# A selective scan laid out with four states of 32 channels on the partitions instead of two states of 64

## The chip, the cores and the metric

The kernel runs on one core of a Trainium2 chip. The metric is the device time of one execution in microseconds (us), as the median of several runs; the core has five engines that matter here: TensorE (PE), VectorE (DVE), ScalarE (ACT), GpSimd (POOL) and the DMA engines, whose transfers SyncE (SP) issues. Tiles on the chip lie in SBUF or PSUM; in both kernels those that TensorE's matmuls write are the ones in PSUM.

## The reference, cut to what matters

A network of four layers on four images of 56 x 56 x 96. Nearly all of the time goes to the selective scan of layers 0 and 1: per image four directions over L = 3136 positions, for 192 channels and 16 states.

```python
def selective_ssm(dtw, dtb, xw, A_log, D, seq):
    xz = jnp.einsum('bld,kd->blk', seq, xw)
    dt_raw, b_ssm, c_ssm = ...                       # 12 (layer 1: 6), 16 and 16 columns of xz   [cut]
    dt = jax.nn.softplus(jnp.einsum('blr,dr->bld', dt_raw, dtw) + dtb)
    a = -jnp.exp(A_log)
    d_a = jnp.exp(dt[..., None] * a)
    d_b = dt[..., None] * b_ssm[:, :, None, :]
    def step(h, inp):
        da_t, db_t, x_t, c_t = inp
        h = da_t * h + db_t * x_t[..., None]
        y_t = jnp.einsum('bds,bs->bd', h, c_t)
        return (h, y_t)
    ...
    return jnp.swapaxes(ys, 0, 1) + seq * D
```

Per state and channel the work is an exp (`da`), a product (`dt*u` with B), a scan over positions (h), a product with C and a sum over the 16 states. Layer norms, convolutions, linear attention and an fp8 feed-forward surround it; the kernel runs them beside the scans of another image ("the other work" below).

## The kernel before

A sequence is cut into chunks of CS = 784 positions. A **unit** is one tile of 128 partitions: 64 channels (one of NG = 3 groups) by 2 states, for one chunk; 16 states make NQ = 8 units per group, 3072 units in all.

```python
    def spread_b(self, ch, q):                       # B of two states onto 128 partitions
        ps = self.psum.tile([128, 1024], F32, tag="b", name="b", bufs=2)
        w = self.sel[:, q].rearrange("p s d -> p (s d)")
        for s in (slice(0, 512), slice(512, CS)):
            self.nc.tensor.matmul(ps[:, s], w, ch.bc[:, s], start=True, stop=True)   # bf16, three terms
        return ps[:, :CS]
    ...
        for n, (ch, g, q) in enumerate(units):       # in scans()                           [cut]
            da = sp.tile([128, CS], F32, name="da", bufs=3)
            nc.scalar.activation(da, ch.dt[g], AF.Exp, scale=ch.na[:, g, q : q + 1])
            db = b
            nc.vector.tensor_tensor(db, ch.du[g], db, ALU.mult)          # in place in PSUM
            if n + 1 < len(units):
                b = self.spread_b(units[n + 1][0], units[n + 1][2])
            if late is not None:
                self.add_up(*late)
            hs = sp.tile([128, CS], F32, name="hs", bufs=2)
            at = ch.carry[:, g, q : q + 1]
            nc.vector.tensor_tensor_scan(
                hs[:, way], da[:, way], db[:, way], at if ch.step else 0.0, ALU.mult, ALU.add
            )
            if ch.step < NCS - 1:
                nc.scalar.copy(at, hs[:, end : end + 1])
            hc = sp.tile([128, CS], F32, name="hc", bufs=2)
            nc.gpsimd.tensor_tensor(hc, hs, ch.cc[q // 2][:, q % 2], ALU.mult)
            late = (ch, g, q, hc)
            yield ch                                 # the caller now emits a share of the other work
    ...
    def add_up(self, ch, g, q, hc):                  # sum over the states, in PSUM         [cut]
        for h in range(2):
            nc.tensor.matmul(
                self.y[64 * h : 64 * h + 64, :HC], self.two, hc[:, h * HC : (h + 1) * HC],
                start=q == 0, stop=False,
            )
```

The scan reads `da` from SBUF and `db` from PSUM.

## Time and profile before

| | before |
|---|---|
| time | 12854.27 us, median of 3 runs (12810.35 to 12864.53); 12832.31 with the run taken beside the change |
| head, loop of scans, tail | 147, 12127, 594 us |
| loop per three units ("a round" below) | 11.84 us |
| TensorE, VectorE, GpSimd, ScalarE busy | 83%, 70%, 54%, 51% |
| scan | 3072, mean 1.82 us |

Read it from the top down: the busy shares say that no engine is full; the groups say which instructions fill each engine and what their engine waited for; dividing the loop by 1024 gives the number that everything below is compared with. The lines themselves stand in the prediction.

### The profile page before, as it was taken

Reading aid. Unit: us, or ns where it says so; the run is one execution under the profiler, and the core shown is the slowest. Engines: PE = TensorE matmul, PEld = TensorE weight load, DVE = VectorE, ACT = ScalarE, POOL = GpSimd, SP = SyncE. Lnnn points to the kernel's source line nnn. Section 1 sums busy time; section 2 is a strip of 40 time slices with the busy share of each in tenths; the row PEclk is TensorE's granted clock in tenths of the full one; section 3 lists DMA queues with packets and bytes.
Section 4 is the critical chain, followed back from the end, with each engine's and each line's share of the span. In section 5 each row is a group of like instructions: output and inputs, shape, how many; then the busy total and the mean of one; then the engine's idle time right before and its main releaser. Section 6 shows DMA issues by size and latency. Waiting matters only on the chain. (4 is left out here: it accounts for less than half of the span.)

```text
span 12868.3 us, 101763 instructions
## 1 busy us (share of the span) xinstructions
PE 10724.2 (83%) x32510; PEld 3416.3 (27%) x32510; DVE 9010.8 (70%) x7546; ACT 6582.8 (51%) x10422; POOL 6985.7 (54%) x3964
## 2 busy tenths in 40 slices
PE   7888888987789878897889888888888888888786
PEld 3222122222223122231223223321233213332143
DVE  4776777667776777767776666877668776777722
ACT  4655555555555555555555544445444454445511
POOL 4555656556554665546555555556555565555510
PEclk6766667766667667776767677766777667776665
DMA  3221212112211221212222121211212122211110
GB/s 84 61 59 46 69 45 54 49 41 68 57 48 50 57 67 42 57 44 65 50 54 53 37 68 49 52 45 41 62 49 52 41 50 61 51 43 40 41 33 28
DMA packets 233374, 662.64 MB, mean 51 GB/s; under 512 B 60866, under 2 KB 141252, under 8 KB 231204
## 3 DMA queue, kind: packets, MB, share of 16 engines
q1 hardware_dynamic: 232064, 654.32, 20.6%
q8 instruction: 257, 4.21, 0.1%
q14 instruction: 281, 2.30, 0.1%
q10 hardware_dynamic: 772, 1.80, 0.1%
HBM read 548.41 MB, written 107.58 MB: 51 GB/s over the span
## 5 line engine op out<-in xcount | busy, mean ns | idle before, releaser
L537 POOL TENSOR_TENSOR hc<-hs,cc 128x784 f32<-128x784 f32 x3072 | 5704.9, 1870 | 4545.8 <-DVE hs L531 3550.0
L551 PE MATMUL y<-hc,two 128*64 128x392 f32 x12288 | 4120.3, 740 | 1294.4 <-POOL hc L537 1219.0
L524 DVE TENSOR_TENSOR b<-du,b 128x784 f32<-128x784 f32 x3072 | 2963.4, 970 | 2481.5 <-PE b L483 2468.6
L531 DVE TENSOR_TENSOR_SCAN hs<-da,carry,b 128x784 f32<-128x784 f32 x2304 | 4166.1, 1834 | 149.4 <-ACT da L522 91.7
L522 ACT ACTIVATE da<-dt,na 128x784 f32<-128x784 f32 x3072 | 2862.0, 945 | 728.9 <-DVE hs L531 714.1
L483 PE MATMUL b<-bc,sel 96*128 96x512 bf16 (+1 forms) x6144 | 2110.7, 436 | 489.9 <-DVE hs L531 486.3
L551 PEld LDWEIGHTS y<-hc,two 128*64 128x64 f32 x12288 | 839.8, 178 | 3117.3 <-POOL hc L537 2320.1
L535 ACT COPY carry<-hs 128x1 f32<-128x1 f32 x2304 | 431.8, 189 | 2140.9 <-DVE hs L531 2134.1
L531 DVE TENSOR_TENSOR_SCAN hs<-da,b 128x784 f32<-128x784 f32 x768 | 1346.3, 1774 | 54.4 <-ACT da L522 21.5
L483 PEld LDWEIGHTS <-sel 96*128 96x128 bf16 x6144 | 457.7, 108 | 3176.4 <-DVE hs L531 1322.1
L431 PE MATMUL ps<-U,wd 64*108 64x392 f32 (+1 forms) x1536 | 864.0, 774 | 0.0
L461 POOL TENSOR_TENSOR du<-dt,U 128x784 f32<-128x784 f32 x384 | 783.0, 2047 | 147.0 <-ACT dt L456 138.9
L593 POOL TENSOR_TENSOR rs<-rs,power 112x4 f32<-112x4 f32 x252 | 257.4, 1021 | 964.6 <-ACT rs L592 784.8
L455 PE MATMUL ps<-dtr,wd 12*128 12x392 f32 (+1 forms) x1536 | 752.5, 736 | 9.4 <-ACT dt L456 3.6
L652 PE MATMUL ps<-win,dg 64*64 64x220 f32 (+9 forms) x2016 | 689.5, 496 | 0.0
L522 ACT ACT_TABLE_LOAD x511 | 655.6, 1283 | 8.3
L568 ACT COPY Ya<-y 64x392 f32<-64x392 f32 x512 | 348.3, 680 | 550.8 <-PE y L565 476.6
L596 PE MATMUL ps<-ident,rs 112*96 112x112 f32 x2016 | 423.6, 376 | 202.8 <-POOL rs L593 202.0
L456 ACT ACTIVATE dt<-ps,wd 128x392 f32<-128x392 f32 x768 | 426.8, 585 | 288.8 <-PE ps L455 279.7
L456 ACT ACT_TABLE_LOAD x339 | 434.9, 1283 | 78.9 <-PE ps L455 73.7
L596 PEld LDWEIGHTS ps<-ident,rs 112*96 112x96 f32 x2016 | 349.2, 250 | 395.4 <-POOL rs L593 308.0
L652 PEld LDWEIGHTS ps<-win,dg 64*64 64x64 f32 (+2 forms) x2016 | 337.1, 175 | 353.9 <-issue 258.7
(215 smaller groups left out, 6739.9 us busy)
## 6 DMA issues: line engine op xcount, KB each, us to landing
cc<-cd SPq DMA_DIRECT2D x1024, 392.0 KB, 5.2
U<-u SPq DMA_DIRECT2D x64, 588.0 KB, 7.9
u<-w SPq DMA_DIRECT2D x56, 224.0 KB, 2.8
z<-w SPq DMA_DIRECT2D x56, 224.0 KB, 2.7
y<-Ya SPq DMA_DIRECT2D x8, 1568.0 KB, 7.0
w<-y SPq DMA_DIRECT2D x56, 224.0 KB, 3.9
w<-z SPq DMA_DIRECT2D x56, 224.0 KB, 4.0
wd<-in_wd_dram SPq DMA_DIRECT2D x32, 367.5 KB, 3.5
```

The source lines that it names most:

```text
L431: nc.tensor.matmul(ps[:m, :HC].rearrange("p (a b) -> p a b", b=HS), self.wx[rows, g, :m], self.in_order(self.U[rows, g], orient, c * CS + ...
L455: nc.tensor.matmul(ps[:, :HC], wt[rows, g], dtr[rows], start=True, stop=True)
L456: nc.scalar.activation(dt[:, h * HC : (h + 1) * HC], ps[:, :HC], AF.Softplus, bias=dtb[:, g : g + 1])
L461: nc.gpsimd.tensor_tensor(du.rearrange("p (a b) -> p a b", b=HS), ch.dt[g].rearrange("p (a b) -> p a b", b=HS), self.in_order(self.U[:, g] ...
L483: self.nc.tensor.matmul(ps[:, s], w, ch.bc[:, s], start=True, stop=True)
L522: nc.scalar.activation(da, ch.dt[g], AF.Exp, scale=ch.na[:, g, q : q + 1])
L524: nc.vector.tensor_tensor(db, ch.du[g], db, ALU.mult)
L531: nc.vector.tensor_tensor_scan(hs[:, way], da[:, way], db[:, way], at if ch.step else 0.0, ALU.mult, ALU.add)
L537: nc.gpsimd.tensor_tensor(hc, hs, ch.cc[q // 2][:, q % 2], ALU.mult)
L551: nc.tensor.matmul(self.y[64 * h : 64 * h + 64, :HC], self.two, hc[:, h * HC : (h + 1) * HC], start=q == 0, stop=False,)
L596: nc.tensor.matmul(ps[:, b], rs[:, q : q + 1].to_broadcast([NT, C]), self.ident[:NT, :NT], start=True, stop=True)
L652: self.nc.tensor.matmul(o[:, a - r0 : e - r0, x0:x1], diag[:, tap], win[:, a + dy - lo : e + dy - lo, x0 + dx : x1 + dx], start=n == 0, st ...
```

## The change

The intent is to relieve TensorE and to save instructions. A **round** now holds three tiles with 4 states of 32 channels each, which share one B and one C. So B is spread once for three tiles, C is multiplied in one instruction over all three, and the sums of the three tiles use three column blocks of 32 of the TensorE array; a fourth block is fed so that all four are in use, and its result is not read. `dt` and `du` are computed once per channel and copied onto the four state blocks by way of DRAM. One of the three products with B moves to GpSimd. Products, scans and product with C are all done in place in one SBUF tile `v`. There are 1024 rounds.

```diff
+    def spread(self, ch, e):
+        for n, l in ((0, ch.dt), (1, ch.du)):
+            t = self.sp.tile([128, NG, CS], F32, name="dt" if n == 0 else "du")
+            for s in range(4):
+                self.nc.sync.dma_start(
+                    t[32 * s : 32 * s + 32], ch.dd[e][n].rearrange("(g d) t -> d g t", d=32)
+                )
+            l.append(t)
     def spread_b(self, ch, q):
-        ps = self.psum.tile([128, 1024], F32, tag="b", name="b", bufs=2)
+        ps = self.psum.tile([128, 2, 512], F32, tag="b", name="b", bufs=1)
+        for h in range(2):
+            nc.tensor.matmul(ps[:, h, :HC], self.sel[:, h, q], ch.cf, start=True, stop=True)   # now fp32
+        b = self.sp.tile([128, CS], F32, name="bs", bufs=1)
+        nc.scalar.copy(b.rearrange("p (h t) -> p h t", h=2), ps[:, :, :HC])
+        return ps[:, :, :HC], b
... in scans():
+        def begin(n):
+            ch, e, q = rounds[n]
+            b, bs = self.spread_b(ch, q)
+            v = sp.tile([128, NG, CS], F32, name="v", bufs=3)
+            nc.gpsimd.tensor_tensor(v[:, 2], ch.du[e][:, 2], bs, ALU.mult)
+            return b, v
-            db = b
-            nc.vector.tensor_tensor(db, ch.du[g], db, ALU.mult)
+            for g in range(NG):
+                ...                                   # exp into das[g]
+                if g < 2:
+                    nc.vector.tensor_tensor(          # v[:, g] = du[:, g] * b
+                        v[:, g].rearrange("p (h t) -> p h t", h=2),
+                        ch.du[e][:, g].rearrange("p (h t) -> p h t", h=2), b, ALU.mult,
+                    )
+            if n + 1 < len(rounds):
+                nxt = begin(n + 1)
-            nc.vector.tensor_tensor_scan(
-                hs[:, way], da[:, way], db[:, way], at if ch.step else 0.0, ALU.mult, ALU.add
-            )
+            for g in range(NG):
+                nc.vector.tensor_tensor_scan(
+                    v[:, g, way], das[g][:, way], v[:, g, way], at[:, g : g + 1] if ch.step else 0.0, ALU.mult, ALU.add
+                )
-            nc.gpsimd.tensor_tensor(hc, hs, ch.cc[q // 2][:, q % 2], ALU.mult)
+            nc.gpsimd.tensor_tensor(v, v, cc.unsqueeze(1).to_broadcast([128, NG, CS]), ALU.mult)
... in add_up():
-            nc.tensor.matmul(
-                self.y[64 * h : 64 * h + 64, :HC], self.two, hc[:, h * HC : (h + 1) * HC],
-                start=q == 0, stop=False,
-            )
+            for n, g in enumerate((0, 1, 2, 2)):
+                nc.tensor.matmul(
+                    self.y[32 * n : 32 * n + 32, h, :HC], self.four, v[:, g, h * HC : (h + 1) * HC],
+                    start=q == 0 or n == 3, stop=n == 3,
+                )
... and: general PSUM tiles 3 -> 4; convolutions give way after every third tap; lengths 100, 260 -> 125, 275
```

## The prediction

> **What bounds the kernel now.** I read the page first: the busy shares, then the costliest groups.
>
> ```profile
> PE 10724.2 (83%) x32510; PEld 3416.3 (27%) x32510; DVE 9010.8 (70%) x7546; ACT 6582.8 (51%) x10422; POOL 6985.7 (54%) x3964
> ...
> L537 POOL TENSOR_TENSOR hc<-hs,cc 128x784 f32<-128x784 f32 x3072 | 5704.9, 1870 | 4545.8 <-DVE hs L531 3550.0
> L551 PE MATMUL y<-hc,two 128*64 128x392 f32 x12288 | 4120.3, 740 | 1294.4 <-POOL hc L537 1219.0
> L524 DVE TENSOR_TENSOR b<-du,b 128x784 f32<-128x784 f32 x3072 | 2963.4, 970 | 2481.5 <-PE b L483 2468.6
> L531 DVE TENSOR_TENSOR_SCAN hs<-da,carry,b 128x784 f32<-128x784 f32 x2304 | 4166.1, 1834 | 149.4 <-ACT da L522 91.7
> L522 ACT ACTIVATE da<-dt,na 128x784 f32<-128x784 f32 x3072 | 2862.0, 945 | 728.9 <-DVE hs L531 714.1
> ```
>
> The reader is to see a loop of 3072 units (exp, product with B, scan, product with C, sum) in which no engine is full. TensorE is nearest, at 83%; VectorE's long idle time ends on TensorE (its product waits 2468.6 us for the B broadcast), GpSimd's on the scan. So the bound is the in-order round trip PE, DVE, POOL, PE with TensorE as its fullest member. In the view of the scan's line the first scan starts at 147.1 us and the last at 12272.6: head 147 us, loop 12127 us, tail after the last scan 594 us. I count in rounds of three units, since the changed kernel works in them: 12127/1024 = 11.84 us per round. The chain of waits at its end spreads over many lines of 1% and names no single culprit.
>
> Then I asked the views of single lines what an instruction of VectorE costs beside GpSimd, because the change moves operands from PSUM to SBUF.
>
> ```profile
> L531 DVE TENSOR_TENSOR_SCAN hs<-da,carry,b x2304: 1811/1839/1850, 235.2 to 12272.6; 128x784 f32<-128x784 f32 x192
> ```
> ```profile
> L788 DVE TENSOR_TENSOR w<-w,ps x28: 602/605/614, 7545.9 to 12538.3; 64x448 f32<-64x448 f32 x28
> ```
> ```profile
> L704 DVE TENSOR_TENSOR w<-w x28: 588/608/2260, 1628.1 to 6782.2; 64x448 f32<-64x448 f32 x28
> ```
> ```profile
> L818 DVE SCALAR_TENSOR_TENSOR w<-w,c,win x28: 654/656/4555, 7596.3 to 12565.5; 96x448 f32<-96x448 f32 x28
> ```
>
> The numbers after the count are shortest, median and longest ns. The scan (da in SBUF, b in PSUM) and L788 (w in SBUF, ps in PSUM) never vary, though GpSimd is busy 54% of the time. L704 and L818, with both inputs in SBUF, take up to 2260 and 4555 ns. The timeline says where the 4555 comes from, VectorE first, then GpSimd in the same stretch:
>
> ```profile
> 7870.43 4.55 DVE L818 SCALAR_TENSOR_TENSOR w<-w,c,win 96x448 f32<-96x448 f32 x1
> ```
> ```profile
> 7869.85 1.01 POOL L593 TENSOR_TENSOR rs<-rs,power 112x4 f32<-112x4 f32 x1 [5.12 <-ACT rs L592]
> 7870.82 3.68 POOL L537 TENSOR_TENSOR hc<-hs,cc 128x784 f32<-128x784 f32 x2
> ```
>
> L818 starts while GpSimd works, stands through a power and two whole products until GpSimd ends at 7874.50, and ends 0.48 us after it: its own work alone. It is a lock, not a sharing of rate, and GpSimd keeps it from one instruction to the next if its queue is full.
>
> [...] This trace agrees for tensor_tensor and scalar_tensor_tensor (608 to 2260, 656 to 4555 ns); a scan with two SBUF inputs is not in it. [...] The trace has 1862 ns (median) for 784 elements[...]. [...] matmuls in different column groups run together. The trace agrees for two groups: 12288 L551 records of 740 ns would be 9.1 ms one after another and cover 4120.3 us.
>
> **The change part by part,** per round (three groups, one state quarter; 1024 rounds).
>
> TensorE. Sums: now four L551 records per unit cover 4120.3/3072 = 1.34 us, 4.02 per round. Then 16 records in fours; if four run together as two do now, 4 x 0.67 = 2.7 us. B: now 2110.7/1024 = 2.06 us per round in bf16; then two fp32 matmuls of 392 columns on the full array, 4 records of about 0.51 us (L609's 195.8 us over 336 records of 448 columns, scaled), 2.0 us: no gain. The projection goes from 12 to 8 records per chunk (864 to about 400 us in all), the step sizes from 6 matmuls to 4 (752 to 500 us). Sum: 10.7 - 1.35 - 0.1 - 0.45 - 0.25 = about 8.6 ms.
>
> ScalarE. Gone are the casts of B, cf and dtr copies (about 0.6 ms) and two thirds of the carries (432 to about 150 us); new are 1024 PSUM copies of 784 columns, about 0.8 us each (448 columns take 0.52[...]), 0.85 ms. About level at 6.5 ms.
>
> DMA. dt and du go to DRAM and back, four ways: 128 x 16 loads of 301 KB = 616 MB and 154 MB of stores onto 662 MB. The queue's share of 20.6% roughly doubles, issued a round or more ahead of use: hidden.
>
> VectorE, own work: 2 of 3 products stay, 2963 to 1976 us, the `rest` subtraction (140) goes: 9010 to about 7.9 ms.
>
> GpSimd, own work: the product with C as one of 2352 elements[...] instead of 3 x 1.86; plus one product with B, 1.86; plus two `du` products per chunk instead of three (256 x 2.04 = 0.52 ms), minus the bf16 correction (213 us). 7.12 us a round, about 8.1 ms in all.
>
> By these sums the fullest engine falls from 10.7 to 8.6 ms. But the scan now reads da and v, **both in SBUF**. If the lock holds for it, scans and GpSimd's instructions exclude each other and their times add:
> - three scans, started 1.74 us apart as in back-to-back pairs now (3.58 us for two, 1.84 for one): 5.2 us
> - product with C 5.26, product with B 1.86: 7.1 us
> - du: 0.52 ms/1024 = 0.51 us
> - the powers (257.4 us): 0.25 us
> - VectorE's other users[...] (L703, L704, L818, L862 and the fp16 steps at L853, L854, L861, unblocked about 226 us): 0.22 us
>
> Sum 13.3 us a round against 11.84 now. The two products from PSUM on VectorE (1.94 us) [...] hide under the C product; exps (2.8 us) and the B copy hide there too. I add 0.15 us for the handoff from scan to GpSimd, which waits for the last scan: 13.45 x 1024 = 13.77 ms, plus head and tail 0.74: **14.5 ms**, 13% slower.
>
> **Rivals.**
> A. The scan does not take the lock. At 1.84 us for 784 elements it runs at about half the rate of the product (0.97)[...] and no scan of this kind is in the trace. Then engines overlap, the fullest has 8.6 ms, and at today's 83% the time is 8.6/0.83 = 10.4 ms. For it speaks only that gap; against it, that two different opcodes with two SBUF inputs block for whole instructions.
> B. Lock plus stalls. B's PSUM tile has one buffer, so B for the next round starts after this round's products, then needs TensorE (2 us), the ScalarE copy (0.85) and the GpSimd product, behind convolutions and table loads (1283 ns each[...]). Where this arrives later than the scans end, nobody holds the lock. At 1 us a round: 15.6 ms.
> C. The lock, but cheaper: in blocked handoffs the fixed part is hidden (L818 needs 0.48 us after GpSimd instead of 0.66). With element time alone, scans 3 x 1.63 (an estimate: 1.84 less some 0.2 fixed)[...], rest 0.4: 12.5 us a round, 12.8 + 0.74 = 13.5 ms. Still slower.
> D. DMA or the one issuing queue holds it up: the spreads wait for stores that wait for GpSimd. They have a round of some 13 us for transfers that land in 5.2 us (392 KB) now; I give it little.
>
> **Range and chances.** B to C span 13.5 to 15.6 ms, and A is a separate heap at 10 to 11 ms to which I give 13%. I take 13.3 to 15.6 ms. Faster 0.14 (A), same 0.06 (all of C's savings and some of the scans slipping in unblocked), slower 0.80.
>
> **What would show it.** In the changed kernel the scan's mean rises far above 1.84 us, shortest near 1.75 and longest several us; GpSimd's product of 784 elements varies too. GpSimd's unblocked time plus unblocked scan time fills some 90% of the loop. TensorE's busy time falls to about 8.6 ms and yet nothing is gained. If the scan's shortest and longest are again within 0.1 us, the lock step is wrong and the time is A's. If scan and GpSimd times fit but the sum leaves over 1 us a round, it is B. If the sums at L551's successor cover clearly more than 2.7 us a round, four column groups do not run together.

## The result

| | before | changed |
|---|---|---|
| median | 12832.31 us (4 runs, 12782.0 to 12864.53) | 16234.17 us (4 runs, 16228.19 to 16246.59) |
| ratio | | 1.2657 (95%: 1.261 to 1.2704) |
| granted TensorE clock, profiled run | 0.689 | 0.666 |
| head and tail, loop | 741, 12127 us | 751, 15481 us |
| loop per round | 11.84 us | 15.12 us |
| mean scan | 1.82 us | 3.32 us |

The four runs of the kernel before lie within 0.7% of one another. A ratio here is worked out from the runs and not from the quoted medians, so it isn't quite their ratio.

The page of the changed kernel, first its busy shares, then the groups that answer to those of before (busy us, mean ns, then the idle time of the engine just before them and what ended most of it):

```profile
PE 9275.2 (57%) x33022; PEld 3530.1 (22%) x33022; DVE 12479.8 (77%) x6273; ACT 5525.5 (34%) x7879; POOL 9306.5 (57%) x2680
...
L560 DVE TENSOR_TENSOR_SCAN v<-da,carry,v 128x784 f32<-128x784 f32 x2304 | 7528.1, 3317 | 165.6 <-ACT da L548 139.3
L568 POOL TENSOR_TENSOR v<-v,cc 128x2352 f32<-128x2352 f32 x1024 | 5917.5, 5780 | 355.6 <-ACT carry L566 219.7
L521 POOL TENSOR_TENSOR v<-du,bs 128x784 f32<-128x784 f32 x1024 | 2367.9, 2312 | 4045.7 <-ACT bs L485 2842.3
...
L584 PE MATMUL y<-v,four 128*32 128x392 f32 x16384 | 2719.9, 745 | 2916.4 <-POOL v L568 2301.8
L483 PE MATMUL b<-cf,sel 128*128 128x392 f32 x4096 | 2571.4, 770 | 2499.7 <-DVE v L551 2499.6
L551 DVE TENSOR_TENSOR v<-du,b 128x784 f32<-128x784 f32 x2048 | 1885.0, 959 | 1605.9 <-ACT bs L485 761.0
```

Here the reader sees TensorE fall from 10724 to 9275 us of work, as intended, and VectorE rise to 12480 us although it has fewer instructions. The rise sits in one place: 2304 scans with carry that took 4166 us now take 7528. TensorE's new waits end on GpSimd's product (L568) and on VectorE's (L551); it isn't the bound any more.

The views of the scan's and the C product's line give the shortest, median and longest duration of one instruction, in ns:

```profile
L560 DVE TENSOR_TENSOR_SCAN v<-da,carry,v x2304: 1812/1840/12768, 261.2 to 15629.7; 128x784 f32<-128x784 f32 x192
...
L560 DVE TENSOR_TENSOR_SCAN v<-da,v x768: 1756/1783/8884, 150.3 to 15311.1; 128x784 f32<-128x784 f32 x192
```
```profile
L568 POOL TENSOR_TENSOR v<-v,cc x1024: 5122/5161/11168, 155.7 to 15631.6; 128x2352 f32<-128x2352 f32 x171
```

The median scan is as it was (1840 ns against 1839), and the longest is seven times as long. So the scan isn't slower; some scans stand. The timeline shows where, in an ordinary stretch (start us, duration us, engine, instruction):

```profile
5012.84 11.73 DVE L560 TENSOR_TENSOR_SCAN v<-da,carry,v 128x784 f32<-128x784 f32 x3
5012.94 6.69 POOL L568 TENSOR_TENSOR v<-v,cc 128x2352 f32<-128x2352 f32 x1
...
5019.60 3.33 POOL L521 TENSOR_TENSOR v<-du,bs 128x784 f32<-128x784 f32 x1
...
5026.24 5.32 DVE L560 TENSOR_TENSOR_SCAN v<-da,carry,v 128x784 f32<-128x784 f32 x3
```

In the second round three scans run with GpSimd idle and take 5.32 us. In the first they take 11.73 us, 6.41 more, because GpSimd's two products, 5.16 + 1.88 us of own work by their medians, take their turns between them (7.04 us, less some overlap at the handoffs). GpSimd's 6.69 and 3.33 us in turn are longer than its own work since it stands behind a scan. What one engine does here, the other waits for.

To account for a round I laid the instructions of the trace over one another. "Held" is the time in which a scan, another of the VectorE instructions that the last term of the prediction's sum counts, or a GpSimd instruction is running or standing; "idle" is the rest; and "alone" (from the experiments 11 to 14) is the middle of a pass from which the other work has been moved away.

| per round, us | held | idle | sum |
|---|---|---|---|
| predicted | 13.3 | 0.15 | 13.45 |
| changed kernel | 12.73 | 2.39 | 15.12 |
| changed kernel, rounds alone | 12.34 | 1.13 | 13.48 |

The waits of the changed kernel (us in total, times, longest) name first what lets the lock lie idle most: the copy of B into SBUF.

```profile
ACT da L548 <- DVE v L560: 5082.3, 1433, 12.2
...
POOL v L521 <- ACT bs L485: 2842.3, 478, 12.4
...
DVE v L551 <- ACT bs L485: 761.0, 290, 15.2
```

ScalarE waits 5082 us for scans to free the `da` tiles, which costs little: the scans in turn wait for `da` only 215.5 us (139.3 and 76.2). GpSimd's 2842 us lie mostly beside scans; only 684 us of them lie where the lock is idle. The next largest part of the idle lock, 508 us, ends on ScalarE's bias instruction before GpSimd's power (run 7).

### The profile page after: what moved, and what is told of

It reads as the page before. It is cut to its first block, busy times and chain, and to the rows that moved or that the text cites. A ratio compares the mean times of both kernels' runs of the same rounds, so it can differ in the third digit from the quotient of the medians.

```text
span 16232.6 us, 103602 instructions
## 1 busy us (share of the span) xinstructions
PE 9275.2 (57%) x33022; PEld 3530.1 (22%) x33022; DVE 12479.8 (77%) x6273; ACT 5525.5 (34%) x7879; POOL 9306.5 (57%) x2680
## 3 DMA queue, kind: packets, MB, share of 16 engines
q1 hardware_dynamic: 631424, 1399.75, 34.4%
## 5 line engine op out<-in xcount | busy, mean ns | idle before, releaser
L560 DVE TENSOR_TENSOR_SCAN v<-da,carry,v 128x784 f32<-128x784 f32 x2304 | 7528.1, 3317 | 165.6 <-ACT da L548 139.3
L568 POOL TENSOR_TENSOR v<-v,cc 128x2352 f32<-128x2352 f32 x1024 | 5917.5, 5780 | 355.6 <-ACT carry L566 219.7
L521 POOL TENSOR_TENSOR v<-du,bs 128x784 f32<-128x784 f32 x1024 | 2367.9, 2312 | 4045.7 <-ACT bs L485 2842.3
L584 PE MATMUL y<-v,four 128*32 128x392 f32 x16384 | 2719.9, 745 | 2916.4 <-POOL v L568 2301.8
L483 PE MATMUL b<-cf,sel 128*128 128x392 f32 x4096 | 2571.4, 770 | 2499.7 <-DVE v L551 2499.6
L551 DVE TENSOR_TENSOR v<-du,b 128x784 f32<-128x784 f32 x2048 | 1885.0, 959 | 1605.9 <-ACT bs L485 761.0
L560 DVE TENSOR_TENSOR_SCAN v<-da,v 128x784 f32<-128x784 f32 x768 | 2519.6, 3329 | 76.2 <-ACT da L548 76.2
L483 PEld LDWEIGHTS b<-cf,sel 128*128 128x128 f32 x4096 | 1052.0, 282 | 4041.2 <-issue 3818.1
L485 ACT COPY bs<-b 128x784 f32<-128x784 f32 x1024 | 821.3, 802 | 1077.2 <-PE b L483 1047.9
L453 POOL TENSOR_TENSOR duc<-dtc,U 96x784 f32<-96x784 f32 x256 | 667.4, 2607 | 657.2 <-ACT dtc L443 461.8
```

The source lines that it names most:

```text
L453: nc.gpsimd.tensor_tensor(du.rearrange("p (a b) -> p a b", b=HS), ch.dtc[e].rearrange("p (a b) -> p a b", b=HS), self.in_order(self.U[e], ...
L483: nc.tensor.matmul(ps[:, h, :HC], self.sel[:, h, q], ch.cf, start=True, stop=True)
L485: nc.scalar.copy(b.rearrange("p (h t) -> p h t", h=2), ps[:, :, :HC])
L521: nc.gpsimd.tensor_tensor(v[:, 2], ch.du[e][:, 2], bs, ALU.mult)
L551: nc.vector.tensor_tensor(v[:, g].rearrange("p (h t) -> p h t", h=2), ch.du[e][:, g].rearrange("p (h t) -> p h t", h=2), b, ALU.mult,)
L560: nc.vector.tensor_tensor_scan(v[:, g, way], das[g][:, way], v[:, g, way], at[:, g : g + 1] if ch.step else 0.0, ALU.mult, ALU.add)
```

## The experiments

The theory: scan and GpSimd exclude each other because the scan now has both inputs in SBUF (**the lock**), and the lock is used for only part of the time. The rivals: the scan in place in SBUF costs this for another reason; the B round trip with one PSUM buffer is the main cost; the other work is; a new engine is the bound. Runs 1 to 10 are timed against the kernel before in the same rounds and all are in the fast state; 11 to 14 are single looks whose state is unknown, and only their rounds are used, not their total times. The PSUM tiles of both kernels come to 4096 columns of fp32 (4 x 512 general ones, 1024 for B and 1024 for the sums in the changed kernel). The experiments keep to that total, so several first cut the general tiles from 4 to 2; the first run is the control for that.

**1. Control: two general PSUM tiles.**

```diff
-        return self.psum.tile([128, 512], F32, tag="ps", name="ps", bufs=4)
+        return self.psum.tile([128, 512], F32, tag="ps", name="ps", bufs=2)
```

> Control: the changed kernel with the general PSUM tiles cut from 4 to 2, results right. Needed because the next two runs need two banks. If the general PSUM tiles play no part in the loss, 16.2 to 16.6 ms and the scan's mean stays at 3.3 us. If they do, clearly over 16.6 ms, and the next two runs must be read against this one.

Measured: 16492.54 us, ratio 1.2836 (1.2814 to 1.2857); 15.34 us a round, 12.73 held and 2.61 idle. Two tiles fewer cost about 0.25 ms; the lock's part is the same.

**2. The scan's second input from PSUM.** A constant tile in PSUM takes the place of `v` as second input, all else equal to the control. The result is wrong (the final comparison nevertheless stayed within its tolerance).

```diff
+        still = self.psum.tile([128, 1024], F32, tag="still", name="still", bufs=1)
+        nc.vector.memset(still, 0.01)
                 nc.vector.tensor_tensor_scan(
-                    v[:, g, way], das[g][:, way], v[:, g, way], at..., ALU.mult, ALU.add
+                    v[:, g, way], das[g][:, way], still[:, :CS][:, way], at..., ALU.mult, ALU.add
```

> The control, with the scan's second input read from a constant tile in PSUM in place of v in SBUF: wrong results on purpose, all waits, buffers and instructions as before. Lock theory: the scan's longest is within 0.1 us of 1.85 us, GpSimd's product of 2352 elements stays at 5.1 to 5.3 us, and the time falls to 10.4 to 12.5 ms. Rival (the round trip B, copy, GpSimd product with its single buffers is what costs): the scan shortens but the idle time moves elsewhere, and the time stays above 15 ms.

Measured: 12969.43 us, ratio 1.0095 (1.008 to 1.011), 11.91 us a round. Its page's first line and the line of its scan:

```profile
PE 8727.4 (67%) x33022; PEld 3313.7 (26%) x33022; DVE 7941.9 (61%) x6274; ACT 5613.4 (43%) x7951; POOL 7964.1 (61%) x2680
```
```profile
L562 DVE TENSOR_TENSOR_SCAN v<-da,carry,still x2304: 1810/1822/1849, 246.0 to 12351.0; 128x784 f32<-128x784 f32 x192
```

The longest scan is 1849 ns where it was 12768: one operand moved to PSUM and every blocked scan is gone. The lock is worth 16.49 - 12.97 = 3.5 ms. The second reading is as important: without the lock the changed layout still isn't faster than the kernel before, though TensorE has 2.0 ms less to do and no engine is above 67%. The rival of 10.4 ms in the prediction wouldn't have come true even without the lock. (This run has two general PSUM tiles, which cost 0.25 ms in run 1; with four, and without the lock, the layout wasn't run, and could come out level with the kernel before.)

**3. The third product with B on VectorE** instead of GpSimd, without the copy of B. Results are right.

```diff
-            b, bs = self.spread_b(ch, q)
-            v = sp.tile([128, NG, CS], F32, name="v", bufs=3)
-            nc.gpsimd.tensor_tensor(v[:, 2], ch.du[e][:, 2], bs, ALU.mult)
-            return b, v
+            return self.spread_b(ch, q), sp.tile([128, NG, CS], F32, name="v", bufs=3)
-                if g < 2:
+                if g < 3:
```

> The changed kernel with the third product with B on VectorE as well, no copy of B: one part of the change undone, the lock left in. Lock theory: 1.85 us a round of GpSimd's locked time goes, 1.9 ms, and with it the idle time that waits for the copy of B, some 0.7 ms: 13.4 to 14.4 ms. Rival (VectorE's own work bounds, 12.5 ms busy): 0.96 us a round is added to VectorE, 1 ms: 17 ms or more.

Measured: 14280.67 us, ratio 1.112 (1.11 to 1.114); 13.25 us a round, 11.09 held and 2.15 idle, mean scan 2.73 us. A round is 1.87 us shorter, about the duration of the GpSimd product taken out (1.88 us), and 1.64 of it came out of the held part. The product on GpSimd, with its copy of B, cost 2 ms; on VectorE, reading B from PSUM, such a product takes 0.96 us and never stands (933 to 974 ns in the changed kernel).

**4. All three products into PSUM**, read there by the scan (control's tiles; results right).

```diff
+                db = self.psum.tile([128, 1024], F32, tag="db", name="db", bufs=1)[:, :CS]
+                nc.vector.tensor_tensor(
+                    db.rearrange("p (h t) -> p h t", h=2),
+                    ch.du[e][:, g].rearrange("p (h t) -> p h t", h=2), b, ALU.mult,
+                )
                 nc.vector.tensor_tensor_scan(
-                    v[:, g, way], das[g][:, way], v[:, g, way], at..., ALU.mult, ALU.add
+                    v[:, g, way], das[g][:, way], db[:, way], at..., ALU.mult, ALU.add
```

> The changed kernel with all three products on VectorE and written to PSUM, from where the scan reads them, results right: the change without the second SBUF input. Lock theory: no instruction of the loop holds the lock but GpSimd's, the scan stays within 1.75 to 1.85 us, VectorE's own work is 3 x 0.97 + 3 x 1.75 = 8.2 us a round, and the time is 10.5 to 12.3 ms, faster than the kernel before. Rival (layout or DMA traffic of the change costs): above 13 ms.

Measured: 13966.64 us, ratio 1.087 (1.0854 to 1.0886), 12.87 us a round: the expectation was missed. Two groups of its page:

```profile
L555 DVE TENSOR_TENSOR_SCAN v<-da,carry,db 128x784 f32<-128x784 f32 x2304 | 4252.2, 1846 | 501.0 <-ACT da L543 253.5
L549 DVE TENSOR_TENSOR db<-du,b 128x784 f32<-128x784 f32 x3072 | 3005.6, 978 | 2286.6 <-PE b L483 1857.8
```

The scan is back at 1846 ns, so the lock is gone, with right results this time. But with one `db` tile, products and scans alternate, the last product comes after two scans, and only then may TensorE write the next B: VectorE now waits 1858 us for it. One wait was exchanged for another.

**5. The kernel before, with only its product moved to SBUF.** The scan works in place in `hs`. Results are right.

```diff
-            db = b
-            nc.vector.tensor_tensor(db, ch.du[g], db, ALU.mult)
+            hs = db = sp.tile([128, CS], F32, name="hs", bufs=2)
+            nc.vector.tensor_tensor(db, ch.du[g], b, ALU.mult)
```

> The kernel BEFORE with one thing of the change alone: the product with B goes to SBUF (into the scan's own output tile, the scan runs in place) and not into PSUM; results right, buffers and layout as before. Lock theory: a unit needs the lock for 1.75 (scan) + 1.85 us (product with C), 10.8 us per three units, with du, powers and the correction 11.9; at the 84% at which the changed kernel used the lock 14.1 us, so 14.4 to 15.5 ms, scan's mean above 2.3 us. Rival (the new layout, the DRAM round trip or the fp32 B is what costs): within 2% of 12.85 ms.

Measured: 14683.56 us, ratio 1.1441 (1.1422 to 1.146); 13.61 us per three units, 11.7 held (expected 11.9), 1.91 idle. The product's move to SBUF, without any of the other parts of the change, makes the old kernel 14% slower. It also takes an `hs` tile one instruction earlier, a possible rival. But with two `hs` tiles that round trip is product, scan and product with C, 0.97 + 1.83 + 1.87 us, for two units, so some 7.0 us for three (an estimate from the durations before), far below 13.61. And the lock shows in single instructions: the longest scan goes from 1850 to 3882 ns, the longest product with C from 2492 to 3827. Two groups of its page by form show who stood:

```profile
L530 DVE TENSOR_TENSOR_SCAN hs<-da,carry,hs 128x784 f32<-128x784 f32 x2304 | 4564.6, 2008 | 179.5 <-ACT da L522 161.4
...
L524 DVE TENSOR_TENSOR hs<-du,b 128x784 f32<-128x784 f32 x3072 | 2965.8, 967 | 3690.7 <-POOL hc L536 2730.9 <-PE b L483 564.5 <-ACT carry L534 311.7
```

The mean scan rose only to 2.0 us and not above the expected 2.3: here it is mostly GpSimd that stands (its product's mean goes from 1870 to 2357 ns), and VectorE waits for it by way of the `hs` tile. A mean of the scan alone would have understated the lock; the sum of held time doesn't.

**6. A second B buffer** (control's tiles, `b` with two PSUM buffers; results right).

```diff
-        ps = self.psum.tile([128, 2, 512], F32, tag="b", name="b", bufs=1)
+        ps = self.psum.tile([128, 2, 512], F32, tag="b", name="b", bufs=2)
```

> The control with 2 general PSUM tiles, and the two banks so freed given to a second buffer of B; results right. If the round trip of the single B tile makes the time in which nobody holds the lock (2.6 us a round in the control), that falls below 1.9 us and the time to 15.4 to 15.9 ms, against 16.49 of the control. If that idle time has other sources (powers, step sizes, loads, the order of the queues), the time stays above 16.2 ms.

Measured: 16043.44 us, ratio 1.2501 (1.2479 to 1.2523); 14.92 us a round, idle 2.33. Against the control's 16492.54 the one buffer is worth 0.45 ms, between the two expectations. GpSimd's idle time that ends on the copy of B shrinks; idle lock time that ends on the sums (449 us), on the powers (597 us) and on the transfer of `du` (280 us) takes part of its place.

**7. The powers off GpSimd** (an add and a reciprocal on VectorE; wrong, relative error 1.9). 508 us of the lock's idle time ended on a power that waited for ScalarE, so this asks whether that wait is on the path.

```diff
-        nc.scalar.activation(rs, ps[:NT, :4], AF.Identity, bias=self.eps[eps][:NT])
-        nc.gpsimd.tensor_tensor(rs, rs, self.power[:NT], ALU.pow)
+        nc.vector.tensor_scalar(rs, ps[:NT, :4], eps, None, ALU.add)
+        nc.vector.reciprocal(rs, rs)
```

> The changed kernel with the power -0.5 taken off GpSimd and its bias off ScalarE: two small VectorE instructions, an add from PSUM and a reciprocal, wrong results on purpose. GpSimd's queue stands for 508 us before the power while nobody holds the lock. If that is time of the path, 15.4 to 15.8 ms; if GpSimd would have had nothing else to do, within 1% of 16.23 ms.

Measured: 16134.5 us, ratio 1.2577 (1.2557 to 1.2598), 0.6% less than the changed kernel. That wait isn't what costs the time. With it gone the held time falls from 12.73 to 12.54 us a round, but the idle time rises from 2.39 to 2.51: other waits end later.

**8. Without the unused fourth column block** (results right).

```diff
-            for n, g in enumerate((0, 1, 2, 2)):
+            for n, g in enumerate((0, 1, 2)):
-                    start=q == 0 or n == 3, stop=n == 3,
+                    start=q == 0, stop=False,
```

> The changed kernel without the fourth, unused column block of the sums: 12288 records and not 16384, results right. TensorE is not the bound at 57%, so every theory here expects the time within 1% of 16.23 ms; the busy time of the sums stays near 2.7 ms if column groups run together whatever their number, and falls to 2.0 ms if they take turns.

Measured: 16256.74 us, ratio 1.2672 (1.2651 to 1.2692): the same. The sums' group:

```profile
L584 PE MATMUL y<-v,four 128*32 128x392 f32 x12288 | 2743.2, 753 | 2855.5 <-POOL v L568 2243.9 <-issue 611.3
```

With 12288 matmuls they cover 2743.2 us, with 16384 they covered 2719.9. The fourth block costs no time here, and neither helps nor hurts.

**9. B by DMA**, as C already is, into an SBUF tile `bb`; all three products on VectorE, SBUF times SBUF into PSUM. No TensorE work and no copy for B; results right.

```diff
-        ch.cd = self.dram.tile([NS, CS], F32, tag="cd", name="cd", bufs=3)
+        ch.cd = self.dram.tile([2 * NS, CS], F32, tag="cd", name="cd", bufs=3)
... fetch() loads rows of B the same way into bb; spread_b() and begin() go
+                db = self.psum.tile([128, 1024], F32, tag="db", name="db", bufs=1)[:, :CS]
+                nc.vector.tensor_tensor(db, ch.du[e][:, g], b, ALU.mult)      # scan then reads db
```

> An attempt at a version that beats both, results right: the changed layout, but B comes as C does, by DMA over the partitions into SBUF; the three products go to PSUM and the scan reads them there, so only the products (3 x 0.97 us, two SBUF inputs) and GpSimd share the lock, and TensorE's fp32 spread of B (2.6 us a round) and the copy of B go. Lock theory: 2.9 + 5.2 + 0.8 = 8.9 us a round of lock, VectorE 8.3 us, scan within 1.75 to 1.85 us, the product's mean above 1.5 us since it waits for the 5.2 us product with C: 11.5 to 13.2 ms. Rival: 400 MB more of DMA or the longer waits of the product hold it at 13.5 ms or more.

Measured: 15368.77 us, ratio 1.2006 (1.1988 to 1.2024), a clear miss. Its product's group, and the view of its line with the shortest, median and longest duration:

```profile
L533 DVE TENSOR_TENSOR db<-du,bb 128x784 f32<-128x784 f32 x3072 | 5722.6, 1863 | 466.4 <-DMA bb<-cd 366.4
```
```profile
L533 DVE TENSOR_TENSOR db<-du,bb x3072: 967/983/6006, 152.5 to 14763.0; 128x784 f32<-128x784 f32 x192
```

The product has become the one with two SBUF inputs, and stands behind the 5.2 us C product: mean 1863 ns, against 970 from PSUM before, though its median is 983. The lock was moved from the scan to the product, not removed. Of the two causes that the rival names, these waits show; more DMA isn't the main one, since transfers of B end only 366 us of VectorE's idle time, and run 10 moves as much and is 1.8 ms faster.

**10. The same, with C's product per tile of 784 elements** instead of one of 2352 (results right).

```diff
+                nc.gpsimd.tensor_tensor(v[:, g], v[:, g], cc, ALU.mult)       # inside the loop over g
-            nc.gpsimd.tensor_tensor(v, v, cc.unsqueeze(1).to_broadcast([128, NG, CS]), ALU.mult)
```

> The same with the product with C as three of 784 elements, each behind its own scan, so that GpSimd holds the lock for 1.85 us at a time, beside a scan that doesn't need it; results right. Lock theory: products wait less, 10.5 to 12.3 ms, faster than the kernel before. Rival (DMA, order of queues): same as the run before it.

Measured: 13547.71 us, ratio 1.0585 (1.0567 to 1.0603), 12.49 us a round, also missed.

```profile
L557 PE MATMUL y<-v,four 128*32 128x392 f32 x16384 | 5000.5, 783 | 3924.1 <-POOL v L539 3868.7
...
L533 DVE TENSOR_TENSOR db<-du,bb 128x784 f32<-128x784 f32 x3072 | 3884.4, 1264 | 494.6 <-DMA bb<-cd 398.5
```

Shorter GpSimd instructions between which VectorE can slip in bring the product's mean from 1863 to 1264 ns and the time down by 1.8 ms. TensorE pays: the three tiles now arrive one after another, and the sums cover 5000 instead of 2720 us, so the column blocks run together less (one after another, 16384 records of 783 ns would be 12.8 ms). It is the best version of the new layout with right results, and still slower than the kernel before. Why it misses the expected range isn't separated; most of GpSimd's idle time before its products (2819 of 3665 us) ends on ScalarE's copies of the carry.

**11 and 12. The rounds alone**, of the changed kernel and of the kernel before: the other work is moved out of the rounds, to the end of each pass.

```diff
-    lengths = [120] + 4 * [125] + 3 * [275]
+    lengths = 8 * [0]
```

> The changed kernel with all work beside the scans (projections, convolutions, feed-forward) put off to the end of each pass, so that the first 100 rounds of a pass run alone; results right, the whole longer. To be read from the trace: time of a round in a stretch without other work. If that other work makes the idle lock time (2.4 us of 15.1), a round takes 12.2 to 13.2 us; if the round trip of B does, 14 us or more.

> The same with the kernel before: three units alone, 11.84 us with the other work. If TensorE's 83% is what the other work costs there, 9.5 to 10.5 us alone; if the in-order round trip is, 11 us or more.

Measured, in the middle of a pass: changed 13.46 to 13.49 us a round in every pass (15.12 with the other work), before 10.7 to 10.9, depending on the stretch taken (11.84). Both between the expectations. In the changed kernel the other work adds 1.65 us a round: 0.39 held (12.73 - 12.34) and 1.26 idle. Of the 3.28 us between the two kernels 2.7 are there in the rounds alone. Of the 1.13 us that stay idle in the rounds alone, 0.72 end on the copy of B.

**13. The rounds alone, with two B buffers**, to settle what those 0.72 us are.

```diff
-        return self.psum.tile([128, 512], F32, tag="ps", name="ps", bufs=4)
+        return self.psum.tile([128, 512], F32, tag="ps", name="ps", bufs=2)
-        ps = self.psum.tile([128, 2, 512], F32, tag="b", name="b", bufs=1)
+        ps = self.psum.tile([128, 2, 512], F32, tag="b", name="b", bufs=2)
... and lengths = 8 * [0]
```

> The changed kernel with all other work moved out of the rounds (lengths 0), two B buffers in PSUM and two general PSUM tiles; results stay right. In the rounds alone (e11) the lock was held 12.34 us of 13.48 and idle 1.13, and 0.72 of that ended on the ScalarE copy of B. Theory 'B round trip': with a second B buffer a round alone takes 12.6 to 12.9 us and the product of GpSimd no longer waits for the copy. Theory 'it is replaced': another wait (sums, du, the exps) takes the place, and a round stays at 13.3 us or more. The held part should stay at 12.3 in both.

Measured: 12.68 to 12.72 us a round, 12.2 held and 0.5 idle, as the first theory expected. In the view of GpSimd's B product, in the same stretch of 1200 us, first run 11 and then run 13 (us of idle time, times):

```profile
  ACT bs L485: 305.3, 47
```
```profile
  ACT bs L485: 34.9, 7
```

So without the single buffer and without the other work the rounds are 96% lock (12.2 of 12.7): this is the loop that the prediction worked out. Less the powers and VectorE's other users (0.47 us), which belong to the other work, its 13.45 us is 12.98. Runs 11 and 13 are on two chips, with granted clocks of 0.632 and 0.674 over the whole run, but the four matmuls of B took 2952 and 2953 ns (median) there and 2951 ns in the changed kernel (clock 0.666): the clocks' difference doesn't show in them.

**14. The rounds alone, without the lock** (run 2's edit and `lengths = 8 * [0]`; wrong).

> The scan with a constant in PSUM as second input (no lock; wrong on purpose as in e2), all other work moved out of the rounds. With other work e2 took 11.91 us a round though no engine was above 67%. Theory 'other work delays an in-order chain': alone a round is near its fullest engine, VectorE 7.2 (3 x 1.74 + 2 x 0.97) or GpSimd 7.1 to 7.6, plus some waits: 7.6 to 9.5 us. Theory 'the round's own chain of waits (B, copy, product, scans, C product, buffers)': 10.8 us or more alone too.

Measured: 9.23 to 9.34 us a round, where run 2 took 11.91 with the other work. In a stretch within a pass (us, then busy us and count of each engine, granted clock, DMA share, GB/s):

```profile
3300.00:4000.00 700.00, 443.89 (x1727) 137.94 (x1725) 518.45 (x370) 331.15 (x450) 557.83 (x170) 0.71 0.51 124
```

VectorE is busy 74%, GpSimd 80%. The round's own chain would allow 9.3 us; it is the other work, threaded through the same queues, that stretches it by 2.6 us.

All rounds side by side, us per round (three units):

| | rounds alone | with the other work | other work adds |
|---|---|---|---|
| before | 10.75 | 11.84 | 1.1 |
| new layout, no lock (runs 14, 2) | 9.3 | 11.91 | 2.6 |
| new layout, lock (run 11, changed kernel) | 13.48 | 15.12 | 1.65 |
| new layout, lock, two B buffers (runs 13, 6) | 12.7 | 14.92 | 2.2 |

Within a row both kernels have the same number of general PSUM tiles: three before, four in the third row, two in the second and fourth. Against the fourth row's 14.92 the control with two tiles has 15.34 (run 1).

## Why the prediction was right or wrong

The direction and the mechanism were right, the size was not: 16234 us lies 4% above the top of the range (15600) and 12% above the predicted time.

- **"If the lock holds for it, scans and GpSimd's instructions exclude each other and their times add": right.** Longest scan 12768 ns, shortest 1756, as the test at the end of the prediction asked. Shown by taking one operand to PSUM (run 2: 1849 ns at the longest, 3.5 ms less), by giving the old kernel nothing but this operand (run 5: 14% slower), and by moving the two-SBUF form to another instruction, which then stood (run 9). One detail was not borne out: the prediction read from the trace before that GpSimd keeps the lock from one instruction to the next (L818 stood 4.55 us, through the end of a power and two whole products); in the changed kernel a scan gets in between GpSimd's two products (at 5019.6 us in the stretch shown above). These runs don't settle which engine goes first when both have more to do.
- **The sum of 13.3 us a round: nearly right, 0.6 too large.** Held time is 12.73 us. The C product's median is 5.16 us (predicted 5.26, an estimate: the trace before has no GpSimd product of another length than 784; 1.88 us for 784 and 5.16 us for 2352 elements give 2.09 ns an element here), the GpSimd B product's 1.88 (1.86), three scans 5.3 (5.2). By these medians the sum stays 13.2 to 13.3, so about half a microsecond of the instructions' fixed parts hides in the handoffs, as rival C argued, whose 12.5 us a round was the author's estimate too; that is inferred from the sum and not measured apart.
- **"I add 0.15 us for the handoff": this step failed.** The lock is idle for 2.39 us a round, not 0.15, and that term of the sum, 2.24 us or 2.3 ms, is larger than the whole miss of 1.7 ms: by luck the held part, 0.6 us a round too large, made the miss smaller. The step held that everything without the lock hides under the C product. Of the 2.39 us only 287 us in the whole execution, 0.28 a round, have one of VectorE's PSUM products in them, so those do hide. What doesn't: (a) the round trip of B with one buffer, 0.77 us a round alone (run 13 against 11), 0.42 with the other work (run 6 against 1); (b) the other work, 1.26 us of idle a round (run 11); that the engine which would take the lock next then stands behind something in a queue is argued, and which waits these are isn't shown.
- **Rival B named half of this and made it too small.** It foresaw B's single buffer, with B's trip standing behind convolutions and table loads, and gave stalls 1 us a round in all (15.5 ms by its own sum, where it says 15.6). The buffer's part was about right; what the other work costs besides was missing. By the prediction's own test, over 1 us a round left over, this rival is the one that came true.
- **Why I could have known.** The kernel before had TensorE as its fullest engine at 83%. I used that figure for rival A (8.6/0.83) and not for the main estimate. The lock is used 84% of the loop (12.73 of 15.12). With the 83% of before, 13.3 us would have given 16.0 a round and 17.1 ms; with the held time as it turned out, 12.73/0.83 = 15.3 a round and 16.4 ms. The lock's use is 83 to 86% in the changed kernel and in runs 1, 3, 5, 6 and 7, and 92 and 96% in the rounds alone (runs 11 and 13). That this lies near TensorE's 83% before is an agreement and not a rule that was tested. I treated the sum of exclusive times as the round; it is about the least that a round can take.
- **TensorE "falls to 8.6 ms": 9.3.** The sums are right (2.66 us a round against 2.7: four column blocks run together, 16384 records of 745 ns, 12.2 ms one after another, cover 2719.9 us; runs 8 and 10). B was sized too small: the records of its fp32 matmul are 770 ns and B covers 2571 us, 2.5 us a round against 2.0; I had scaled it from L609, another matmul. It cost nothing here.
- **ScalarE 6.5 ms: 5.5. DMA "roughly doubles": 20.6% to 34.4%.** No queue of it bounds a round: waits on transfers end only some 0.3 us a round of the idle lock.
- **Rival A, 10.4 ms without the lock: wrong too.** It would have been 12.97 ms (run 2). Its round of 9.3 us is there when nothing else runs (run 14), so the new layout without the lock is worth 1.45 us against 10.75 (how much of that is TensorE's relief wasn't separated); the other work then takes 2.6 us instead of 1.1 and uses the gain up. That is where the expected gain of the change would have gone even without the lock.

What stays open: which parts of the other work cost the 1.26 us of idle. The one part tried alone, the powers, is worth 0.6%. And no version was found that beats the kernel before; those with the new layout and right results end at 13.5 ms (run 10).

## What to carry to other kernels

Before moving an operand of a VectorE instruction from PSUM to SBUF while GpSimd works, count the inputs: with two in SBUF its time no longer lay beside GpSimd's here but added to it (12.73 of 15.12 us a round), and long GpSimd instructions made it worse (a VectorE product took 1863 ns in the mean beside C products of 2352 elements and 1264 ns beside those of 784, runs 9 and 10). Take the sum of such exclusive times for about the least that a round can take, and leave room for idle time: here the lock was used for 83 to 86% of a round beside the other work. And test a layout's own loop with the other work taken away: what it gains there can be used up by work in the same queues.
